# Two runs of matmuls joined, and a later start of the exponentials, ahead of a gated cross-attention pipeline

## The chip, the cores and the metric

The kernel runs on one core of a Trainium2 chip. The metric is the device time of one execution in microseconds (us). A core has five engines that run side by side and meet at semaphores: TensorE (PE in the profile; its weight loads are listed apart as PEld), VectorE (DVE), ScalarE (ACT), GpSimd (POOL) and SyncE (SP), which here only issues DMA transfers. Each engine works through its own list of instructions.

## The reference, cut to what matters

All data are float32. `x` has 4 sequences of 2048 tokens with 512 features, and `ctx_768` has 4 contexts of 77 tokens with 384 features.

```python
q = split_heads(layernorm(x) @ Wq)          # 16 heads of 64
k = split_heads(context @ Wk); v = split_heads(context @ Wv)
attn = softmax(einsum('bhid,bhjd->bhij', q, k) * SCALE)
out = einsum('bhij,bhjd->bhid', attn, v)     # heads joined again
x = x + tanh(g_xattn[0]) * (out @ Wo + bo)
x = x + tanh(g_ffn[0]) * (layernorm(x) @ W[idx] + b[idx])   # idx = argmax of logits + gumbel noise
```

The kernel uses that the context is short. For every batch it forms M = Wq·Kᵀ and VO = V·Wo once, so that scores are x·M and the attention output is p·VO.

## The kernel before, in words

**Tiling.** The 8192 tokens are cut into 16 groups of 512, four groups to a sequence. For each group the kernel computes the scores, the softmax, the attention output with its residual and the feed-forward layer. The groups are pipelined: while one group's scores run on TensorE, the softmax of that group or the one before runs on ScalarE, VectorE and GpSimd.

**Seven products.** Every large matmul is done by the class `Seven` (line 452): a 2x2 block product with seven block products in place of eight. `product(s)` issues the matmuls of step s (line 482), and `post(s)` takes the result out of PSUM. There are two ways to do that: a `keep` step is a copy on ScalarE (line 488, with a bias line 492), and an added step is an addition on VectorE (line 506). Steps with the same result slot r write to the same PSUM bank one after the other, so the later one needs the copy of the earlier one first. In the usual order, steps 0 and 2 share slot 0: step 2 accumulates onto what step 0 left, after ScalarE has copied it. Each float32 product of 128x256 shows as two MATMUL instructions.

**Scores.** The scores of a group are made by three such objects: `s0` for the first two pairs of key chunks (8 MATMUL instructions in a step), `s1` for the next two (8) and `s2` for the last one (4). For group 1, six steps of `s0` come first, in an order of their own (`SHORT`, line 460). Then a loop of seven turns issues one step of `s1` and one of `s2` in each turn; behind its first turn it issues the seventh step of `s0`. In `SHORT`, steps 0, 2, 3 and 5 are copied by ScalarE, and steps 1, 4 and 6 are added by VectorE.

**VO.** `build_vo(p, engines)` (line 334) makes VO of two heads, 2p and 2p+1. It has six results (three chunks of rows by two heads), each with one 64-row matmul of 512 columns, which shows as two MATMUL instructions, twelve for a pair (line 343). Each result is scaled on its way from PSUM into a staging slot, by VectorE (line 346) or ScalarE (line 348); the letters of `engines`, taken in turn, say which: "DDA" gives the third and the sixth result to ScalarE, "D" none. Four DMA transfers, issued by SyncE, then take the pair to DRAM (lines 352 and 353). Heads from 2 on rotate through five staging slots, so head 13 takes the slot of head 8. `load_vo(0)` (line 359) reads batch 0's part of VO back, once all are stored.

**Softmax.** For group 0, `head_max(0, h)` on VectorE (lines 544 and 546) makes the negated maxima of a set of four heads. `exps(0, n0, n1)` on ScalarE (line 552) makes 64 exponentials, 16 for each set; those of set h need `head_max(0, h)`. `head_sum` (VectorE, line 559) and `head_scale` (GpSimd, line 563) follow, and then `p_columns` (VectorE, line 572).

**PSUM and order.** Seven PSUM banks are handed out in rotation (`bank`, line 88). While `s0` keeps its first bank, six rotate. The kernel is written under a manual schedule: the order of the calls is the order on each engine. The stage around the change is written by hand on lines 764 to 791: VO of pairs 3 to 7 stands between the steps of group 1's scores, while the exponentials of group 0 fill ScalarE. The list `e` says how many exponentials come by the end of each turn of the loop. The last of the 64 stand ahead of `s1.post(0)` on ScalarE (lines 791 to 797).

Of the kernel before, what the change touches and what calls it, by code (L numbers as in the profile page):

```python
# [19 lines left out]
def flamingo_block_kernel(  # L20
# [34 lines left out]
    NT, D = x.shape  # L55
# [32 lines left out]
    def bank(name):  # L88
        return pm.tile([P, 512], F32, tag="mm", name=name)
# [29 lines left out]
    def weight_sum(w, n, engine=None):  # L119

        to, a, b_, op = ((5, 0, 3, ALU.subtract), (3, 3, 2, ALU.add), (4, 3, 0, ALU.subtract),
                         (6, 1, 4, ALU.subtract))[n]
        (engine or nc.gpsimd).tensor_tensor(flat(w[:, to]), flat(w[:, a]), flat(w[:, b_]), op)
# [65 lines left out]
    def by_chunk(t):  # L189

        return t.rearrange("p (a q e) -> p q a e", a=NA, e=32)

    def chunked(t):
        return t.rearrange("p (q a e) -> p q a e", a=NA, e=32)
# [61 lines left out]
    def v_cols(p, at, n):  # L256
        return vT_f[:, ds(p * BP + at, n)] if p < 7 else wf_f[:, ds(6 * D + at, n)]
# [72 lines left out]
    def stage_of(h):  # L330

        return vo_st[h if h < 2 else 2 + (h - 2) % (len(vo_st) - 2)]

    def build_vo(p, engines):
        n = 0
        for c in range(3):
            r = min(P, BP - c * P)
            for hh in range(2):
                stg = stage_of(2 * p + hh)
                hr = ts(hh, DH)  # L340
                ps = bank("ps_vo")

                nc.tensor.matmul(ps, v_cols(p, c * P, P)[hr], wo[hr, p, :], start=True, stop=True)  # L343
                src, dst = by_chunk(ps[:r, :]), chunked(stg[:r, c, :])
                if engines[n % len(engines)] == "D":
                    nc.vector.tensor_scalar(dst, src, tgx[:r], None, ALU.mult)
                else:
                    nc.scalar.activation(dst, src, AF.Copy, scale=tgx[:r])
                n += 1
        for hh in range(2):  # L350
            d, stg = vo_d[2 * p + hh], stage_of(2 * p + hh)
            nc.sync.dma_start(out=d[0 : 2 * P].rearrange("(c r) e -> r c e", r=P), in_=stg[:, 0:2])
            nc.sync.dma_start(out=d[2 * P :], in_=stg[: BP - 2 * P, 2])
# [5 lines left out]
    def load_vo(bi):  # L359
        src = vo_d.rearrange("h (r b k) e -> (h r) b k e", b=B, k=NK)[:, bi]  # L360
        for o, c in ((0, 0), (1, 0), (1, 1), (0, 1)):
            nc.sync.dma_start(out=vo[:, BLK[o, c]], in_=src[:, ts(c, KH), ts(o, D // 2)])
# [174 lines left out]
    def head(i, h):  # L537
        return sc[i][:, h, :, :J]
# [3 lines left out]
    def head_max(i, h):  # L542
        mx = stat[:, ds((16 + h) * NG, NG)]
        nc.vector.tensor_reduce(mx, head(i, h), AX.X, ALU.max)  # L544
        nmx[h] = small.tile([P, NG], F32, tag=f"nmx{h}", name="nmx")
        nc.vector.tensor_tensor(nmx[h], mx, norms[i].down, ALU.mult)  # L546

    def exps(i, n0, n1):

        for n in range(n0, n1):  # L550
            h, g = n // NG, n % NG
            nc.scalar.activation(head(i, h)[:, g, :], head(i, h)[:, g, :], AF.Exp,  # L552
                                 scale=norms[i].up[:, g : g + 1], bias=nmx[h][:, g : g + 1])
# [3 lines left out]
    def head_sum(i, h):  # L557
        sums[h] = sm = small.tile([P, NG], F32, tag=f"sm{h}", name="sm")
        nc.vector.tensor_reduce(sm, head(i, h), AX.X, ALU.add)  # L559
        nc.vector.reciprocal(sm, sm)  # L560

    def head_scale(i, h):
        nc.gpsimd.tensor_tensor(head(i, h), head(i, h), sums[h].unsqueeze(2).to_broadcast([P, NG, J]),  # L563
                                ALU.mult)
# [115 lines left out]
    def centre_wf(wfr, c):  # L680
        nc.gpsimd.tensor_tensor(wfr[:, c, :], wfr[:, c, :], wf_mean, ALU.subtract)
        for o in range(2):
            nc.gpsimd.tensor_scalar(chunked(wf[:, BLK[o, c // 2], c % 2, :]), by_chunk(wfr[:, c, :])[:, ts(o, 2)],
                                    tgf, None, ALU.mult)
# [79 lines left out]
    head_max(0, 0)  # L764
    build_vo(3, "AAD")
    head_max(0, 1)
    exps(0, 0, 8)
    e = (8, 16, 24, 32, 41, 50, 57)
    for s in range(6):
        s0.product(s)  # L770
        s0.post(s)
        if s < 2:
            centre_wf(wfr, 2 * s)
            centre_wf(wfr, 2 * s + 1)
        if s == 2:
            weight_sum(wf, 0)
            weight_sum(wf, 1)
        if s == 3:
            weight_sum(wf, 2)
        if s < 4:  # L780
            build_vo(4 + s, "DDA" if s < 2 else "D")
        if s < 2:
            head_max(0, 2 + s)
        exps(0, e[s], e[s + 1])
        if s == 3:
            weight_sum(wf, 3)
            load_vo(0)
        if 3 <= s:
            head_sum(0, s - 3)
            head_scale(0, s - 3)  # L790
    exps(0, 57, 64)
    for s in range(7):
        s1.product(s)
        s2.product(s)
# [32 lines left out]
    for i in range(1, NGRP):  # L827
# [69 lines left out]
        for s in range(7):  # L897
# [12 lines left out]
            if 1 <= s:  # L910
                e = (0, 10, 20, 32, 44, 56, 64)
# [225 lines left out]
```

## Time and profile before

| what | value |
|---|---|
| median of three runs | 1242.3 us (1242.0 to 1243.12) |
| the profiled execution, whole time | 1242.8 us |
| its span, first to last instruction | 1241.0 us, so 1.8 us lie around it |
| TensorE busy | 1231.3 us (99% of the span) |
| VectorE, GpSimd, ScalarE busy | 904.9, 894.0, 684.9 us |
| mean granted TensorE clock | 0.998 |

The table is read as follows. A busy share is an average over all stages. The engine with the highest share need not set the end in each of them, and busy TensorE is not TensorE at its peak, because the ends of matmuls are modelled. So the chain of work that ended last is read next, and then the instructions of the one stage that the change touches, from about 87 to 133 us.

### The profile page before, as it was taken

The page shows a single profiled execution, that of the slowest core. Times are in us where ns is not written, and L with a number is a line of the kernel's source. Part 1 is how long each engine was busy: PE and PEld are TensorE (multiplying, and loading weights), DVE is VectorE, ACT ScalarE, POOL GpSimd, SP SyncE. Part 2 cuts the span into 40 slices and gives each one's busy share as a digit, 9 for nine tenths or more (in the row PEclk, how much of TensorE's full clock was granted, in tenths as well). Part 3 has the DMA queues.
Part 4 walks back from the last instruction along what each step waited for, and adds up shares of the span by engine and source line. Part 5 has one row for each costly group of instructions (what it writes and reads, how often), then busy time and mean ns, then how long its engine had stood idle before and what let it go on. Part 6 is the DMA issues. An engine that isn't in the chain of part 4 may idle for free.

```text
span 1241.0 us, 17016 instructions
## 1 busy us (share of the span) xinstructions
PE 1231.3 (99%) x5704; PEld 1063.2 (86%) x5704; DVE 904.9 (73%) x1843; ACT 684.9 (55%) x1970; POOL 894.0 (72%) x493
## 2 busy tenths in 40 slices
PE   9999999999999999999999999999999999999997
PEld 6676888888888888888888888888888888888886
DVE  6788977666877766677776767776776877666576
ACT  4648545548273564827356482745638274563824
POOL 5559885758957775785968778575977877585666
PEclk9999999999999999999999999999999999999999
DMA  9868200314023030304006030202304121010102
GB/s 269 324 194 286 32 1 1 68 47 107 1 62 92 1 69 1 69 22 125 8 1 153 1 69 1 56 14 85 68 1 111 43 52 17 1 35 1 35 1 68
DMA packets 94486, 80.28 MB, mean 65 GB/s; under 512 B 3888, under 2 KB 81584, under 8 KB 94400
## 3 DMA queue, kind: packets, MB, share of 16 engines
q1 hardware_dynamic: 92128, 76.61, 24.2%
q10 hardware_dynamic: 1664, 1.47, 0.4%
q0 software_dynamic: 608, 1.13, 0.2%
q8 instruction: 45, 0.74, 0.2%
q14 instruction: 41, 0.34, 0.1%
HBM read 44.07 MB, written 35.13 MB: 64 GB/s over the span
## 4 chain that ended last, share of the span: by engine, by line
PE 96%; DVE 2%; ACT 0%; DMA 0%; POOL 0%; issue 0%; DVEq 0%
PE ps_s L482 39%; PE ps_a L482 37%; PE ps_f L482 15%; PE ps_kv L269 2%; PE ps_vo L343 2%; PE ps_m L307 1%; DVE s L377 1%; ACT t L606 0%; DMA m<-in_Wk_dram 0%; POOL r L405 0%; DVE t L424 0%; DVE r L400 0%; DVE y L424 0%; DVE snap L506 0%; DVE y L602 0%
## 5 line engine op out<-in xcount | busy, mean ns | idle before, releaser
L482 PE MATMUL ps_a<-pT,vo 128*128 128x256 f32 x2240 | 486.2, 379 | 0.0
L482 PEld LDWEIGHTS ps_a<-pT,vo 128*128 128x128 f32 x2240 | 425.6, 190 | 57.9
L552 ACT ACTIVATE s<-s,nmx,up 128x77 f32<-128x77 f32 x1024 | 355.8, 445 | 1.6 <-DVE nmx L546 1.6
L444 POOL TENSOR_TENSOR pT<-pT 128x1280 f32<-128x1280 f32 x64 | 185.8, 2904 | 171.1 <-PE ps_a L482 164.4
L482 PE MATMUL ps_s<-tq,m 128*128 128x256 f32 x1280 | 290.6, 380 | 0.0
L482 PEld LDWEIGHTS ps_s<-tq,m 128*128 128x128 f32 x1280 | 242.6, 190 | 36.0 <-issue 1.5
L488 ACT COPY snap<-ps_s 128x512 f32<-128x512 f32 (+1 forms) x188 | 93.6, 514 | 291.1 <-DVE t L424 131.1
L482 PE MATMUL ps_s<-xc,m 128*128 128x256 f32 x960 | 221.1, 379 | 0.0
L482 PEld LDWEIGHTS ps_s<-xc,m 128*128 128x128 f32 x960 | 182.2, 190 | 27.4 <-issue 1.2
L563 POOL TENSOR_TENSOR s<-s,sm 128x1232 f32<-128x1232 f32 x64 | 145.2, 2269 | 47.4 <-DVE sm L560 47.3
L506 DVE TENSOR_TENSOR snap<-snap,ps_s 128x512 f32<-128x512 f32 (+1 forms) x141 | 83.7, 594 | 126.6 <-PE ps_s L482 121.6
L482 PE MATMUL ps_f<-tq,wf 128*128 128x256 f32 x512 | 118.3, 379 | 0.0
L572 DVE STREAM_TRANSPOSE pT<-s 128x512 f32<-128x512 f32 x160 | 101.1, 678 | 15.8 <-POOL s L563 15.8
L444 POOL TENSOR_TENSOR tq<-xc,tq 128x512 f32<-128x512 f32 x64 | 85.2, 1332 | 34.9 <-PE ps_f L482 32.4
L405 POOL TENSOR_TENSOR r<-r,neghalf 32x16 f32<-32x16 f32 (+1 forms) x33 | 93.1, 2831 | 21.9 <-DVE r L400 21.3
L482 PEld LDWEIGHTS ps_f<-tq,wf 128*128 128x128 f32 x512 | 97.3, 190 | 13.2
L559 DVE TENSOR_REDUCE sm<-s 128x16 f32<-128x1232 f32 x64 | 91.5, 1429 | 21.9 <-ACT s L552 21.9
L535 DVE STREAM_TRANSPOSE s<-snap 128x512 f32<-128x512 f32 x156 | 99.9, 685 | 6.1 <-ACT snap L488 3.8
L544 DVE TENSOR_REDUCE ps_st<-s 128x16 f32<-128x1232 f32 x64 | 92.4, 1444 | 2.1
L482 PE MATMUL ps_f<-xc,wf 128*128 128x256 f32 x384 | 90.7, 379 | 0.0
L444 POOL TENSOR_TENSOR tq<-xc 128x512 f32<-128x512 f32 x64 | 81.4, 1272 | 7.2 <-DVE xc L419 5.8
L488 ACT COPY snap<-ps_f 128x512 f32<-128x512 f32 x63 | 36.9, 585 | 86.8 <-PE ps_f L482 86.8
(142 smaller groups left out, 1183.5 us busy)
## 6 DMA issues: line engine op xcount, KB each, us to landing
xg<-in_x_dram SPq DMA_DIRECT2D x64, 256.0 KB, 5.9
out_dram<-y SPq DMA_DIRECT2D x60, 256.0 KB, 4.8
vo<-vo_d SPq DMA_DIRECT2D x16, 640.0 KB, 5.6
m<-m_d SPq DMA_DIRECT2D x12, 640.0 KB, 4.2
vo_d<-vo SPq DMA_DIRECT2D x14, 512.0 KB, 4.2
m_d<-vo SPq DMA_DIRECT2D x4, 960.0 KB, 6.4
wq<-in_WqT_dram SPq DMA_DIRECT2D x8, 256.0 KB, 4.9
wq<-in_Wo_dram SPq DMA_DIRECT2D x1, 2048.0 KB, 13.7
```

The costliest lines, as they stand in the source:

```text
L269: nc.tensor.matmul(ps[:, :BJ], w[:, c, ts(p, P)], cR[:, c].rearrange("p b j -> p (b j)"), start=(c == 0), stop=(c == NCC - 1))
L405: nc.gpsimd.tensor_tensor(r, r, neghalf[:32, : r.shape[1]], ALU.pow)
L444: (engine or nc.gpsimd).tensor_tensor(self.at[name], self.at[a], self.at[b_], op)
L482: nc.tensor.matmul(self.ps[r][:, n, :], self.w(blk, c, pair), self.cols(cname, c), start=(first and n == 0 and c == 0), stop=(c == h - 1), ...
L488: nc.scalar.copy(dst, self.ps[r])
L506: nc.vector.tensor_tensor(c, c, self.ps[r], ALU.add)
L535: nc.vector.transpose(key_chunk(sc[i], k), cols.rearrange("p (g h r) -> p g h r", h=HA, r=R))
L544: nc.vector.tensor_reduce(mx, head(i, h), AX.X, ALU.max)
L552: nc.scalar.activation(head(i, h)[:, g, :], head(i, h)[:, g, :], AF.Exp, scale=norms[i].up[:, g : g + 1], bias=nmx[h][:, g : g + 1])
L559: nc.vector.tensor_reduce(sm, head(i, h), AX.X, ALU.add)
L563: nc.gpsimd.tensor_tensor(head(i, h), head(i, h), sums[h].unsqueeze(2).to_broadcast([P, NG, J]), ALU.mult)
L572: nc.vector.transpose(pT[i].all[:, k, :].rearrange("p (g h r) -> p g h r", h=HA, r=R), key_chunk(sc[i], k))
```

## The change

Only the stage on lines 764 to 791 is changed.

- Behind step 0 of group 1's scores, VO of pair 4 is no longer made. Steps 0 and 1 of `s0` follow each other on TensorE.
- Behind step 1, VO of pair 4 and then of pair 5 are made, both with the pattern "DDA". Two exponentials stand ahead of pair 4 on ScalarE, six between the pairs and two behind them. `head_max(0, 2)` stands behind both pairs.
- Behind step 2, two exponentials come first. Then comes VO of pair 6, now with the pattern "DDA" instead of "D", so that two of its six results go to ScalarE. Then come `head_max(0, 3)` and eight exponentials.
- Pair 7 stays behind step 3 with the pattern "D".
- The exponentials are spread in another way: 4 stand ahead of the loop (8 before), 18 are issued by the end of the turn of step 1, 28 by that of step 2, 38, 48 and 56 by those of steps 3, 4 and 5 (before: 16, 24, 32, 41, 50 and 57 by the ends of the six turns). The rest, now 8 and before 7, follows the loop as before.

The number of instructions of each kind is the same, but for two scalings that move from VectorE to ScalarE.

```diff
-    exps(0, 0, 8)
-    e = (8, 16, 24, 32, 41, 50, 57)
+    exps(0, 0, 4)
+    e = (4, 8, 18, 28, 38, 48, 56)
     for s in range(6):
         s0.product(s)
         s0.post(s)
...
-        if s < 4:
-            build_vo(4 + s, "DDA" if s < 2 else "D")
-        if s < 2:
-            head_max(0, 2 + s)
-        exps(0, e[s], e[s + 1])
+        if s == 1:
+            exps(0, 8, 10)
+            build_vo(4, "DDA")
+            exps(0, 10, 16)
+            build_vo(5, "DDA")
+            head_max(0, 2)
+            exps(0, 16, e[2])
+        else:
+            e0 = e[s]
+            if s == 2:
+                exps(0, e0, e0 + 2)
+                e0 += 2
+            if s in (2, 3):
+                build_vo(4 + s, "DDA" if s == 2 else "D")
+            if s == 2:
+                head_max(0, 3)
+            exps(0, e0, e[s + 1])
...
-    exps(0, 57, 64)
+    exps(0, 56, 64)
     for s in range(7):
         s1.product(s)
         s2.product(s)
```

## The prediction

> **What bounds the kernel now.** I read the page's busy shares first, then the chain that ended last in order of time, then the timeline of ScalarE in the changed stage. The chain is TensorE nearly throughout, so only what TensorE waits for, or spends itself, counts. Its pieces (start, us, what) in the stage:
>
> ```profile
> 48.20 7.72 PE ps_vo L343 x36
> 87.33 2.77 PE ps_vo L343 x12
> 90.10 1.93 PE ps_s L482 x8
> 92.03 2.77 PE ps_vo L343 x12
> ...
> 108.90 23.51 PE ps_s L482 x108
> 132.41 30.22 PE ps_a L482 x140
> 162.63 10.36 PE ps_f L482 x48
> ```
>
> The reader is to see that short runs are dear: a matmul costs 7.72 / 36 = 0.214 us in a long VO run and 10.36 / 48 = 0.216 in a long run of products, but twelve in a run of their own take 2.77 (not 2.57) and eight take 1.93 (not 1.73). Each start of a run costs 0.20 us.
>
> The timeline of ScalarE has start, duration, line, tiles, count, and in brackets idle time with who ended it:
>
> ```profile
> 93.97 0.69 ACT L348 ACTIVATE vo<-ps_vo,tg 128x512 f32<-128x512 f32 x1
> 94.88 0.68 ACT L348 ACTIVATE vo<-ps_vo,tg 64x512 f32<-64x512 f32 x1 [0.21 <-PE ps_vo L343]
> 98.67 0.69 ACT L348 ACTIVATE vo<-ps_vo,tg 128x512 f32<-128x512 f32 x1 [0.38 <-PE ps_vo L343]
> 99.62 0.68 ACT L348 ACTIVATE vo<-ps_vo,tg 64x512 f32<-64x512 f32 x1 [0.26 <-PE ps_vo L343]
> 106.16 0.59 ACT L488 COPY snap<-ps_s 128x512 f32<-128x512 f32 x1
> 106.64 5.59 ACT L552 ACTIVATE s<-s,nmx,up 128x77 f32<-128x77 f32 x16
> 118.09 0.57 ACT L488 COPY sn<-ps_s 128x512 f32<-128x512 f32 x1
> 121.22 0.58 ACT L488 COPY sn<-ps_s 128x512 f32<-128x512 f32 x1 [1.35 <-PE ps_s L482]
> ```
>
> ScalarE idles 0.85 us between 88.42 and 118.09. The copy at 118.09 is `s1.post(0)`, ending at 118.66. TensorE's timeline says when it is needed:
>
> ```profile
> 112.39 4.48 PE L482 MATMUL ps_s<-xc,m 128*128 128x256 f32 x20
> 116.71 5.34 PE L482 MATMUL ps_s<-tq,m 128*128 128x256 f32 x24
> ```
>
> The 24 are steps 1 and 2 of `s1` and `s2`. Step 2 of `s1` starts behind twelve of them, at 116.71 + 12 x 0.216 = 119.30, and needs that copy. So the cover is only 0.64 us. This is the narrow place.
>
> **The change part by part.** *Two starts of runs go.* Between VO of pair 3 and the long run there are nine starts now and seven afterwards: -2 x 0.20 = -0.40 us, all on the path. New starts by the same rows: steps 0 and 1 at 90.03, pairs 4 and 5 at 90.03 + 1.93 + 1.73 = 93.69, step 2 at 93.69 + 2.77 + 2.57 = 99.03, pair 6 at 100.96, step 3 at 103.73, pair 7 at 105.66, the long run at 108.43 (108.83 now).
>
> *VectorE.* A scaling takes 4.03 / 6 = 0.67 us. In a VO run the two heads come together: the first two results are there 1.16 us after the start (102.52 against 101.36 in pair 6 now), the next two at 2.01, the last two at 2.9. VectorE, done with `s0.post(1)` at 94.5 (step 1 ends at 93.7, 0.2 later its addition starts, 0.63), has pair 4's four scalings done at 97.5 and pair 5's at 100.2, `head_max(0, 2)` (1.43 + 0.17) at 101.8. It waits for pair 6 until 102.12 and so keeps up. With six banks in rotation, pair 5's first two matmuls want, at 96.46, the banks that pair 4's first scalings leave at 95.5 and 96.2. That fits by 0.2; if the weight load waits, it costs at most the 0.20 of a start. Bounds 0 and 0.2; I take 0.1, the margin being as large as the cost. Pair 6's two scalings off VectorE buy nothing, as it waits for pair 7's first result (105.66 + 1.16 = 106.82) anyway.
>
> *Queues.* Pair 4's and 5's stores are issued one to three us later. Head 13 in pair 6 wants the slot of head 8, whose last store is issued at about 97.6. Stores of this size landed after 2.3 to 3.8 us in the stage, so at 101.4 at the latest, before the 102.8 of the first scaling. Pair 7's last store comes 0.4 earlier, and with it `load_vo(0)`: no gain, since the loaded part is first read on TensorE at 132. GpSimd gets no new step before the last `head_scale`.
>
> *ScalarE, the step that decides.* An exponential costs 0.343 us in sequence ((5.59 - 0.445) / 15, with 0.445 the mean of one), a scaling 0.575 (four from 88.42 to 90.72), a copy 0.48 (106.16 to 106.64). Behind pair 6's run start (100.96), the last result comes at 103.86. Walking the queue up to there: four exponentials end at 92.1, copy, four and two more by 94.7; the third result of pair 4 comes only at 95.7 (idle 1.0), the sixth at 96.6 (idle 0.3); six exponentials, two scalings, two exponentials to 101.1, a copy, two exponentials to 102.3; pair 6's third result at 102.97 (idle 0.7), its sixth at 103.86 (idle 0.3). Idle time is 2.4 us, not 0.85, and there are two scalings more. From 103.86: scaling 0.575, 44 exponentials 15.1, the copies of steps 3 and 5 0.96, so `s1.post(0)` starts at 120.5 (118.09 now) and ends at 121.07. Behind `s1.post(0)` ScalarE has slack again (1.35 us of idle before 121.22 now).
>
> TensorE wants that copy at 119.30 - 0.40 = 118.90. It gets going after 121.07, plus 0.05 for the semaphore (the chain's issue pieces are 0.02 to 0.07) and up to 0.20 for the weight load, which can't be hidden after a wait. I take 0.25 in all, the row of a run's start being the nearest; with both at nothing the wait is 2.17. So a wait of 2.4 us appears where there was none: +2.4.
>
> *What the later end of the exponentials does next.* The last `head_sum`, `head_scale`, `p_columns` move by 2.4, and TensorE behind them by 2.0, so relative to it they lose 0.4. The nearest need is step 6 of `s1` at 129.66 now, on a bank that VectorE leaves at 127.5: cover 2.1, so nothing.
>
> *Sum*: -0.40 + 2.42 + 0.1 = +2.1 us. Against the profiled execution that is 1242.8 + 2.1 = 1244.9; that execution lies 0.5 above the median, so the forecast is 1242.3 + 2.1 = 1244.4. No change from which a measurement of this kernel could tell it is about 0.2%, or 2.5 us (1244.8): the forecast lies just inside.
>
> **The clock.** TensorE never stands still for microseconds in the stages before the end, so the one row is the end. The stretches, with granted clock in the third column from the right:
>
> ```profile
> 1232.00:1233.00 1.00, 0.63 (x3) 0.20 (x2) 0.96 (x4) 0.92 (x5) 1.00 (x2) 1.00 0.00 0
> 1234.00:1235.00 1.00, 0.00 (x0) 0.00 (x0) 0.90 (x2) 0.00 (x0) 0.92 (x2) 1.00 0.46 104
> 1235.00:1236.00 1.00, 0.00 (x0) 0.00 (x0) 0.87 (x2) 0.00 (x0) 0.90 (x1) 0.52 0.85 170
> ```
>
> The last matmul ends at 1232.63 and the clock is halved from about 1235.04, 2.4 us later: just the length of the wait above. The price of a fall is bounded by the start of the kernel: the first 48 projections take 13.66 us against 12.64 for the next 48, 1.02 lost, and the six warm-up matmuls take 2.93 against 1.29 at full rate, 1.64 lost. Bounds 1.0 and 2.7; I take 1.7, in the middle.
>
> The Trainium skill, "TensorE: Matmul & The Clock Gate", section "HAM oscillation — how this bites in real kernels", asks for no TensorE gap beyond some 3.4 us, and counts the half clock in windows of that length. By it this gap costs nothing and the sum stays at 1244.4; an estimate from its figure for one window at half clock is 1.7 lost. The row, with a fall after 2.4 us, differs and speaks against the change.
>
> **Rivals.** *The clock falls in the new wait.* For it: the 2.4 us above. Against it: the moment of counting may lie unfavourably, and a fall needs nearly the whole gap. It decides once the gap passes about 2.4 us in one count. 1244.4 + 1.7 = 1246.1, slower.
>
> *The cover holds.* If step 2 of `s1` didn't wait for that copy, or ScalarE made up its idle time, the two starts are all: 1242.3 - 0.4 = 1241.9. For it: no TensorE wait on ScalarE is seen now. Against: 118.66 lies ahead of 119.30 now, so none could be seen.
>
> *A staging store is late.* Pair 6's sixth result on ScalarE belongs to head 13. If head 8's store lands after 103.86, every later exponential slips by the excess; from 0.4 us on the whole is slower than 0.2%, and with 1 us it is 1245.4. Against: that needs 6.3 us to land, and 3.8 is the longest in the stage.
>
> **How the numbers follow.** Wait without a fall of the clock 0.47, own range 1243.7 to 1245.2, of which 0.36 lies inside 0.2% and 0.11 above it, where ScalarE is later by another 0.4; clock falls 0.36; cover holds 0.10; late store 0.05; a gain beyond 2.5 us, for which no row speaks, 0.02. Faster 0.02, same 0.36 + 0.10 = 0.46, slower 0.11 + 0.36 + 0.05 = 0.52. The range leaves out the held cover below and about 0.08 above: 1242.9 to 1246.8 (the top is 1244.4 with a fall at 2.4, between the 1.7 taken and its bound of 2.7).
>
> **What would show it.** Right: vo runs of 24 in the chain; ScalarE's copy of `s1.post(0)` near 120.5; a TensorE gap of about 2.4 us ahead of step 2 of `s1`, released by ACT; everything later shifted by the same 2.1. Wrong: no such gap, a granted clock under 1.00 near 122, or ScalarE idle behind pair 6.

## The result and the profile after

The changed kernel takes 1245.71 us (median of 13 executions, 1244.4 to 1247.48), the one before 1243.12 us (13 executions, 1242.0 to 1243.73). The ratio is 1.0025, with a 95% interval of 1.0018 to 1.0033. So the change costs some 3 us (2.6 by the medians, 3.1 by the ratio). The profiled execution after has a span of 1243.9 us, 2.9 us more than that of before.

Single executions of one kernel differ by a microsecond or more at their start, far ahead of the change: the first 48 projections took 13.66 us in the profile of before, 12.83 in that of after and up to 14.89 in the profiles further down. So the profiles are compared over one stretch, called the stage here. It runs from the first matmul of pair 3's VO to the first matmul of step 1 of group 0's feed-forward layer. Both points are read from TensorE's timeline. (In the chain, a piece that nothing released begins at the modelled end of the piece before it: for the kernel before 0.07 and 0.17 us later than the matmuls at these two points.)

The chain of the profile after in order of time (start, us, what):

```profile
86.57 2.78 PE ps_vo L343 x12
89.35 3.65 PE ps_s L482 x16
93.00 5.39 PE ps_vo L343 x24
98.39 1.93 PE ps_s L482 x8
100.32 2.82 PE ps_vo L343 x12
...
119.87 0.47 ACT sn L488
120.35 0.04 issue
120.39 14.90 PE ps_s L482 x60
135.30 30.22 PE ps_a L482 x140
165.51 10.36 PE ps_f L482 x48
```

The two joined runs are there, and they cost what long runs cost. But the chain now goes through ScalarE, which releases TensorE at 120.39. The ends of the stage in TensorE's timeline of before:

```profile
87.26 2.85 PE L343 MATMUL ps_vo<-wq 64*128 64x512 f32 x12
164.19 2.11 PE L482 MATMUL ps_f<-tq,wf 128*128 128x256 f32 x9
```

And of after:

```profile
86.50 2.85 PE L343 MATMUL ps_vo<-wq 64*128 64x512 f32 x12
167.08 3.62 PE L482 MATMUL ps_f<-tq,wf 128*128 128x256 f32 x16
```

The stage lasts 76.93 us before and, from unrounded starts, 80.57 us after, 3.64 us more. The accounts close: the execution after came to pair 3 by 0.75 us sooner, lost 3.64 us in the stage, and from there to the end both take the same (1076.8 us).

TensorE's timeline of after inside the stage (start, duration, line, tiles, count, and in brackets the idle time ahead, counted from the modelled end of the matmul before, with who ended it):

```profile
115.60 2.75 PE L482 MATMUL ps_s<-tq,m 128*128 128x256 f32 x12
120.39 4.54 PE L482 MATMUL ps_s<-tq,m 128*128 128x256 f32 x12 [2.04 <-ACT sn L488]
124.77 2.75 PE L482 MATMUL ps_s<-xc,m 128*128 128x256 f32 x12
```

The 24 matmuls of steps 1 and 2, one run before, are cut in two by a wait for ScalarE's copy. And the second twelve take 4.54 us where the first take 2.75. The stretches of the same profile (length, then busy time and count of PE, PEld, DVE, ACT, POOL, then granted clock, DMA share, GB/s) say why:

```profile
118.00:119.00 1.00, 0.35 (x2) 0.00 (x0) 0.00 (x0) 1.00 (x4) 0.62 (x1) 1.00 1.08 336
119.00:120.00 1.00, 0.00 (x0) 0.00 (x0) 0.10 (x1) 1.00 (x4) 0.00 (x0) 1.00 1.05 353
120.00:121.00 1.00, 0.61 (x2) 0.58 (x3) 1.00 (x1) 1.00 (x4) 0.00 (x0) 0.85 1.04 362
121.00:122.00 1.00, 1.00 (x4) 0.73 (x4) 0.59 (x2) 0.35 (x2) 0.23 (x1) 0.50 1.07 359
122.00:123.00 1.00, 1.00 (x4) 0.82 (x3) 0.00 (x0) 0.00 (x0) 1.00 (x1) 0.50 1.15 322
123.00:124.00 1.00, 1.00 (x4) 0.82 (x3) 0.00 (x0) 0.06 (x1) 1.00 (x2) 0.50 1.23 185
124.00:125.00 1.00, 1.00 (x6) 0.81 (x6) 0.93 (x2) 0.56 (x2) 1.00 (x2) 0.94 1.24 177
```

From about 120.7 to 124.1 the granted clock is 0.50: a row then counts four matmuls, with those that its edges cut, and six at full clock.

ScalarE's own timeline of after shows where it lost its time:

```profile
94.95 0.69 ACT L348 ACTIVATE vo<-ps_vo,tg 128x512 f32<-128x512 f32 x1 [0.98 <-PE ps_vo L343]
95.85 0.68 ACT L348 ACTIVATE vo<-ps_vo,tg 64x512 f32<-64x512 f32 x1 [0.21 <-PE ps_vo L343]
102.27 0.69 ACT L348 ACTIVATE vo<-ps_vo,tg 128x512 f32<-128x512 f32 x1 [0.64 <-PE ps_vo L343]
103.17 0.68 ACT L348 ACTIVATE vo<-ps_vo,tg 64x512 f32<-64x512 f32 x1 [0.21 <-PE ps_vo L343]
119.77 0.57 ACT L488 COPY sn<-ps_s 128x512 f32<-128x512 f32 x1
```

It idles 0.98 us ahead of pair 4's third result, and 0.64 ahead of pair 6's third, which it didn't scale before; with the two gaps of 0.21 that is 2.04 us, against 0.85 before. The copy of step 0 of `s1` starts 33.27 us behind pair 3's VO in the timelines (119.77 - 86.50); before it was 30.83 (118.09 - 87.26).

### The profile page after: what moved, and what is told of

It is laid out like the page before. It is cut to its first block, busy times and chain, and to the rows that moved or that the text cites. A ratio compares the mean times of both kernels' runs of the same rounds, so it can differ in the third digit from the quotient of the medians.

```text
span 1243.9 us, 17018 instructions
## 1 busy us (share of the span) xinstructions
PE 1232.0 (99%) x5704; PEld 1066.2 (86%) x5704; DVE 904.0 (73%) x1841; ACT 686.0 (55%) x1972; POOL 894.0 (72%) x493
## 4 chain that ended last, share of the span: by engine, by line
PE 95%; DVE 2%; ACT 2%; DMA 0%; POOL 0%; issue 0%; DVEq 0%
PE ps_s L482 38%; PE ps_a L482 37%; PE ps_f L482 15%; PE ps_kv L269 2%; PE ps_vo L343 2%; PE ps_m L307 1%; ACT s L552 1%; DVE s L377 1%; ACT t L606 0%; DMA m<-in_Wk_dram 0%; POOL r L405 0%; DVE t L424 0%; DVE r L400 0%; DVE y L424 0%; DVE snap L506 0%
```

## The experiments

The theory to test first was that the copy of step 0 of `s1` comes too late and nothing else, and that the clock falls because of the wait. The table gives all runs. All times are counted from the first matmul of pair 3's VO, and all but those of before are differences to before, in us. "Last sum" is the start of the last `head_sum` of group 0, which follows the last exponential. "Attention" is the first matmul of group 0's attention output; the expectations below end their stage there (45.08 us before, by the chain). "Stage" is the stretch defined above, and "lateness" is how much later TensorE is 16 matmuls further on, and stays to its last matmul.

| kernel | last sum | attention | stage | lateness | clock at half in the stage | ratio to before, 95% interval |
|---|---|---|---|---|---|---|
| before | 30.97 | 44.99 | 76.93 | | no | |
| after | +2.43 | +3.64 | +3.64 | +3.64 | yes | 1.0025 (1.0018 to 1.0033) |
| after_again | +2.44 | +3.64 | +3.64 | +3.64 | yes | 1.0027 (1.0018 to 1.0036) |
| e1_copy_first | +3.18 | +1.26 | +2.95 | +3.06 | no | 1.0024 (1.0014 to 1.0034) |
| e2_pair6_vector | +1.01 | +0.53 | +0.79 | +0.89 | no | 1.0008 (0.9999 to 1.0017) |
| e3_pair6_alone | +1.42 | +0.94 | +1.20 | +1.30 | no | 1.0011 (1.0002 to 1.0020) |
| e4_filled_gap | +2.43 | +1.95 | +2.21 | +2.31 | no | 1.0017 (1.0007 to 1.0026) |
| e5_half_wait | +3.18 | +1.26 | +2.95 | +3.06 | no | 1.0024 (1.0014 to 1.0033) |
| e7_exps_behind_copy | +0.74 | 0.00 | +0.52 | +0.62 | no | 1.0004 (0.9995 to 1.0013) |
| e8_joined_refilled | -0.70 | -0.31 | -0.31 | -0.31 | no | 0.9996 (0.9987 to 1.0005) |

The six kernels that wait for the second chain described below lose another 0.10 us between the last two points: sixteen matmuls behind a wait take 3.72 us and not 3.62, twelve 2.86 and not 2.75.

**The copy ahead of the last exponentials.** The change, with this edit:

```diff
-    exps(0, 56, 64)
...
             s1.post(0)
             s2.post(0)
+            exps(0, 56, 64)
```

> Edit: the change, with the last eight exponentials of group 0 put behind the first copies of s1 and s2 on ScalarE. The stage from the start of VO of pair 3 to the start of the attention took 45.08 us before and 48.73 after the change. Theory (ScalarE reaches the copy of step 0 of s1 too late): the copy starts 8 x 0.343 = 2.7 us earlier, no TensorE wait is left at step 2 of s1, the clock stays at 1.00, and only the two saved starts of runs are left: stage 45.08 - 0.40 = 44.7 us, time 0.4 us under before. Rival (the joined runs wait by themselves, on banks or on VectorE): a wait of some 2 us stays and the stage is 47 us or more.

The wait at step 2 did go: steps 1 and 2 are one run again. But the time didn't come back. TensorE's timeline of this kernel:

```profile
116.24 5.34 PE L482 MATMUL ps_s<-tq,m 128*128 128x256 f32 x24
130.69 2.86 PE L482 MATMUL ps_s<-tq,m 128*128 128x256 f32 x12 [1.34 <-DVE sn L506]
167.03 3.72 PE L482 MATMUL ps_f<-tq,wf 128*128 128x256 f32 x16 [1.33 <-POOL tq L444]
```

Two waits stand further down, 1.34 us for VectorE and 1.33 us for GpSimd, and the clock stays at 1.00 behind both. So the first half of the theory, that only the copy counts, fell. The chain of this kernel says what the waits come from:

```profile
118.51 2.76 ACT s L552 x8
121.29 1.45 DVE sm L559
...
123.17 2.27 POOL s L563
125.46 0.50 DVE pT L572
...
142.25 3.54 ACT s L552 x10
...
165.70 1.28 POOL tq L444
166.98 0.04 issue
167.03 8.90 PE ps_f L482 x40
```

It starts at group 0's last exponential and runs on through its sum, its scaling and its transposes, then through group 1's maxima and exponentials, to the column sums of the feed-forward layer on GpSimd. It never touches TensorE for 46 us. The moved exponentials end 0.75 us later than after the change (3.18 against 2.43), because the two copies (0.47 and 0.27) now stand ahead of them. So the edit cured one chain and fed another, which starts on the same engine.

**Half of it.** The change, with only four exponentials moved:

```diff
-    exps(0, 56, 64)
+    exps(0, 56, 60)
...
             s2.post(0)
+            exps(0, 60, 64)
```

> Edit: the change, with only the last four exponentials put behind the first copies of s1 and s2. Theory: the copy comes 1.37 us earlier, TensorE waits 2.2 - 1.37 = 0.8 us, and a wait so short does not halve the clock; stage 45.08 - 0.40 + 0.85 = 45.5 us, time 0.4 us over before. If the clock falls for waits of this length too, the stage is 47.2 us. If the copy is not what is waited for, the stage stays at 48.7 us.

The wait at step 2 was 0.67 us where 0.8 was foreseen, and the clock stayed. But the stage is the same as in the run before to the hundredth, 2.95 us over before. The last exponential ends at the same place in both, and that sets the stage. How TensorE's waits on the way are divided (0.67, 0.41 and 1.32 us here, 1.34 and 1.33 there) doesn't matter.

**Pair 6 by VectorE alone.** The change, with this edit:

```diff
-                build_vo(4 + s, "DDA" if s == 2 else "D")
+                build_vo(4 + s, "D")
```

> Edit: the change, but pair 6 scaled by VectorE alone, as before. Theory: ScalarE saves the two scalings and the waits for them, but then waits for step 3 (there 0.1 us after its run ends), so the copy of step 0 of s1 starts 1.4 us earlier than after the change; TensorE wants it 0.4 us earlier than before and waits 0.8 us; clock 1.00 throughout; stage 45.08 - 0.40 + 0.85 = 45.5 us, time 0.4 us over before. Rival (the joined runs alone make the wait): the wait stays at 2.0 and the stage at 47 to 48.7 us.

The wait at step 2 is 0.62 us, and the attention starts 0.53 us later than before. The theory had 0.45, the rival about 2 us or more. So the joined runs do not make the long wait by themselves, but they are not free: with the exponentials spread as in the change, ScalarE idles 1.87 us and not 0.85 (0.98 and 0.21 at pair 4's results, 0.68 ahead of the copy of step 3), and the last sum comes 1.01 us later. How much of that is due to the joined runs and how much to the spread, this run does not separate.

**Pair 6's scalings alone.** The kernel before, with this edit:

```diff
-            build_vo(4 + s, "DDA" if s < 2 else "D")
+            build_vo(4 + s, "DDA" if s < 3 else "D")
```

> Edit: the kernel before, with the one part that pair 6 is scaled by both engines (DDA). Theory (two chains that begin on ScalarE): the last exponential ends 1.15 + 0.3 = 1.45 us later than before. The copy of step 0 of s1 then ends at about 120.1 where step 2 wants it at 119.30, so TensorE waits 0.8 to 0.9 us; and the chain that goes on from the last exponential (sum, scaling, transposes, group 1's maxima and exponentials, the sums of the feed-forward layer's columns) had only 0.23 us to spare, so by the feed-forward layer's step 1 TensorE is 1.2 us late in all. Clock 1.00 in the stage. Time 1.2 us over before. Rival (only the copy counts): 0.9 us over before, and no wait at the feed-forward layer. Rival (joining the runs is the cause): no change from before.

Here the last sum is 1.42 us later and step 1 of the feed-forward layer 1.20 us, both as expected, with no run joined. The rival in which only the copy counts had 0.9 us and no wait further on: the attention is 0.94 us late, but the delay grows to 1.30 behind step 1, for which TensorE waits on GpSimd. This part (1.42) and that of the rest of the change (1.01) add up to the 2.43 of the whole.

**The second chain alone.** The kernel before, with its last exponentials moved behind the copies:

```diff
-    exps(0, 57, 64)
...
             s1.post(0)
             s2.post(0)
+            exps(0, 57, 64)
```

> Edit: the kernel before, with its last seven exponentials of group 0 put behind the first copies of s1 and s2 on ScalarE; nothing else. Theory (second chain): the copy comes 2.4 us earlier, so it can't be waited for, but the last exponential ends 0.75 us later (two copies stand ahead of it), which exceeds the 0.23 us that the second chain had to spare, so TensorE waits 0.5 us ahead of step 1 of group 0's feed-forward layer, for GpSimd; time 0.5 us over before. Rival (the copy is the only place where ScalarE matters): no wait anywhere, time as before.

The copy comes early here, no run is joined, and every scaling stays where it was. Still TensorE waits, in one place:

```profile
162.75 1.89 PE L482 MATMUL ps_f<-xc,wf 128*128 128x256 f32 x8
165.00 3.72 PE L482 MATMUL ps_f<-tq,wf 128*128 128x256 f32 x16 [0.35 <-POOL tq L444]
```

The last sum is 0.74 us later, and step 1 starts 0.52 us later, as the theory had it. (The 0.35 us in the row count from the modelled end of the matmul before.) So the second chain had 0.22 to 0.23 us to spare in the kernel before. All six experiments that slip and keep the clock agree on it: the stage grows by the slip of the last sum less that much (3.18 to 2.95 twice, 1.01 to 0.79, 1.42 to 1.20, 2.43 to 2.21, 0.74 to 0.52). The time of this kernel by itself (1.0004, with 1 inside the interval) couldn't have told it.

**The wait filled with work.** The change, with unused matmuls in TensorE's wait; nothing is left out, and they add 1.73 us of work:

```diff
     for s in range(7):
+        if s == 2:
+            fill = bank("ps_w")
+            for _ in range(4):
+                nc.tensor.matmul(fill[:, :T2], xc[1]("B11", 0)[:, :P], xc[1]("B11", 0), start=True, stop=True)
         s1.product(s)
```

> Edit: the change, with four unused matmuls of 256 columns (eight MATMUL instructions, 1.73 us) put into TensorE's wait ahead of step 2 of s1; it adds work and leaves the order of all else. Theory (the clock is halved because TensorE stands still for about 2 us): the clock stays at 1.00, step 2 of s1 starts as late as after the change (33.8 us behind the start of pair 3's VO), and the stage takes 48.73 - 1.7 = 47.0 us; the time falls by 1.7 us against the change, to 1.5 us over before. Rival (the slow matmuls behind the wait come from something else, such as the transfers or the weights): stage 48.7 us and time as after the change or more.

TensorE's timeline, with the added matmuls on line 808:

```profile
118.06 2.75 PE L482 MATMUL ps_s<-tq,m 128*128 128x256 f32 x12
120.65 1.89 PE L808 MATMUL ps_w<-xc 128*128 128x256 f32 x8
122.86 2.86 PE L482 MATMUL ps_s<-tq,m 128*128 128x256 f32 x12 [0.31 <-ACT sn L488]
```

Its stretches:

```profile
122.00:123.00 1.00, 0.69 (x4) 0.29 (x3) 0.63 (x1) 1.00 (x4) 0.00 (x0) 1.00 1.09 351
123.00:124.00 1.00, 1.00 (x5) 0.90 (x6) 0.96 (x2) 0.81 (x3) 0.00 (x0) 1.00 1.11 353
124.00:125.00 1.00, 1.00 (x6) 0.87 (x6) 0.09 (x1) 0.11 (x1) 0.77 (x1) 1.00 1.09 351
```

Step 2 starts as late as after the change, 33.89 us behind pair 3's VO in both. But the clock stays at 1.00 and its twelve matmuls take 2.86 us, not 4.54, although the transfers run at 351 to 353 GB/s, within the 185 to 362 of the slow stretches there. So the slow matmuls come from the idle TensorE and not from its neighbours. The attention starts 1.69 us sooner than after the change, where 1.7 was expected. Of that, 1.33 us remain in the end, because the second chain now sets it (2.31 us over before, not 1.95). The times of all executions agree: this kernel's median is 2.28 us over before, that of the changed kernel below 3.67.

**The changed kernel again.** No edit.

> The changed kernel as it is, once more, for the clock. Theory (the clock is judged in stretches of 3.4 us whose start is unrelated to the kernel, and falls when most of one is idle): the same wait of 2.0 to 2.2 us ahead of step 2 of s1, and either again 3.4 us at half clock behind it and a stage of 48.7 us, or none and a stage of 47.0 us; in the second case TensorE waits another 0.3 us at the feed-forward layer's step 1. The times of single runs then lie in two bands some 1.4 us apart, blurred by about 1 us from the kernel's start. Rival (the clock falls in every run): always 48.7 us.

The wait was 2.04 us once more and the clock fell once more, as two of the stretches show:

```profile
121.00:122.00 1.00, 0.50 (x2) 0.48 (x3) 0.99 (x1) 1.00 (x3) 0.00 (x0) 1.00 1.09 353
123.00:124.00 1.00, 1.00 (x4) 0.81 (x3) 0.00 (x0) 0.00 (x0) 1.00 (x1) 0.50 1.11 341
```

It fell 1.4 us behind the end of the wait here and 0.3 us behind it in the first profile, so the moment is not tied to the wait. Yet the stage is 80.57 us in both. It can hardly fall in every execution: both profiles show it, but two of the 24 times of the changed kernel (1244.16 and 1244.4; the others are 1245.48 and more) lie less than 2.5 us above the fastest of before (1242.0), and with a fall 3.64 are lost. In how many it falls stays open; two clear bands were not seen.

**A kernel that keeps the joined runs.** The change, with the stage's lists written anew:

```diff
-    build_vo(3, "AAD")
+    build_vo(3, "AADADD")
...
-    exps(0, 0, 4)
-    e = (4, 8, 18, 28, 38, 48, 56)
+    exps(0, 0, 5)
+    e = (5, 14, 21, 33, 43, 52, 60)
...
         if s == 1:
-            exps(0, 8, 10)
             build_vo(4, "DDA")
-            exps(0, 10, 16)
+            exps(0, 14, 17)
             build_vo(5, "DDA")
             head_max(0, 2)
-            exps(0, 16, e[2])
+            head_max(0, 3)
+            exps(0, 17, 21)
         else:
-            e0 = e[s]
-            if s == 2:
-                exps(0, e0, e0 + 2)
-                e0 += 2
             if s in (2, 3):
-                build_vo(4 + s, "DDA" if s == 2 else "D")
-            if s == 2:
-                head_max(0, 3)
-            exps(0, e0, e[s + 1])
+                build_vo(4 + s, "D")
+            exps(0, e[s], e[s + 1])
...
-    exps(0, 56, 64)
+    exps(0, 60, 64)
```

> Edit: the change's two joined runs, but with pair 6 scaled by VectorE alone, one scaling of pair 3 moved from ScalarE to VectorE (AADADD), the maxima of the sets 2 and 3 both behind pair 5, and the exponentials put where ScalarE idled (5 ahead of the loop, 14, 21, 33, 43, 52 and 60 by the ends of the turns). Theory (both chains begin on ScalarE, and the runs' starts are TensorE's own cost): the last exponential ends 0.8 us earlier than before against the start of pair 3's VO, neither chain is waited for, the clock stays at 1.00, and the stage from pair 3's VO to the attention takes 45.08 - 0.40 = 44.7 us; time 0.4 us under before. Rival (a joined run makes TensorE wait for banks): a wait on VectorE inside the VO of pairs 4, 5 or 7, stage 45.1 us or more.

The chain is TensorE alone again:

```profile
86.52 2.77 PE ps_vo L343 x12
89.29 3.65 PE ps_s L482 x16
92.94 5.39 PE ps_vo L343 x24
...
107.78 23.51 PE ps_s L482 x108
131.29 30.22 PE ps_a L482 x140
```

From pair 3's VO to the attention it is 131.29 - 86.52 = 44.77 us, against 45.08 before: 0.31 of the 0.40 us. The joined VO run takes 5.39 and not 5.34, and pair 7's run 2.82 and not 2.78, some 0.05 us each. The last sum is 0.70 us earlier than before, where 0.8 was expected of the last exponential, and TensorE waits for neither chain. Several things were moved at once here, so this profile shows that the joined runs can be kept without either chain being late, and not which of the moves does it. The median is 1242.31 us against 1242.62 in the same session. That is the expected direction, but the ratio 0.9996 (0.9987 to 1.0005) can't be told from no change. It is plainly faster than the changed kernel (1246.29 there).

## Why the prediction came out as it did

**The time** says less than it seems. 1245.71 us lies inside the stated range, nearer to the rival with a fall of the clock (1246.1) than to the forecast (1244.4). But before itself was measured 0.8 us higher here than in the three runs on which the forecast stands, and the rise of 2.6 to 3.1 us lies between the forecast's 2.1 and the rival's 3.8. What happened is told by the profiles.

**The starts of runs** were right: 3.65 and 5.39 us for the joined runs, 3.66 and 5.34 foreseen. Up to `s1` they save 0.35 us, not 0.40. **ScalarE's queue**, the step that was said to decide, was right to a few hundredths: the copy was put 33.24 us behind pair 3's VO (120.5 - 87.26) and came at 33.27. The four idle times were foreseen as 1.0, 0.3, 0.7 and 0.3 us (2.3 in all, and not the 2.4 of the text, which nothing else uses) and measured as 0.98, 0.21, 0.64 and 0.21. **The wait** was foreseen as 2.42 us and measured as 2.20: step 2 starts 1.85 us later than before, and would have started 0.35 sooner. (The 2.04 in the row count from a modelled end.) The missing 0.22 is the restart: 0.04 us of issue lies between the copy's end and the matmul, not the 0.25 taken. The matmuls behind the wait cost another 0.10, so that the wait by itself makes TensorE -0.35 + 2.20 + 0.10 = 1.95 us late, as the kernel with the filled wait shows at the attention.

**The clock** is where the likeliest case failed. The prediction took the wait without a fall as likeliest (0.47) and the fall as its nearest rival (0.36). The rival is what both profiles of the changed kernel show, and "a granted clock under 1.00 near 122" was among the prediction's own signs of being wrong. The fall cost 3.64 - 1.95 = 1.69 us, as half of the 3.41 us at half clock would (1.71). The 1.7 foreseen hit that, but as the middle of bounds from 1.0 to 2.7, and so with some luck. The step that failed is "a fall needs nearly the whole gap", with 2.4 us as the point of decision: 2.04 us of idle time was enough twice, and 1.34, 0.67 and 0.62 were not. The 2.4 us came from one row at the end of the kernel, and such a row is one draw. In the ten profiles the clock fell between 2.04 us (the second chain alone) and 5.31 us (the kernel that keeps the joined runs) behind the last matmul. The Trainium skill, "TensorE: Matmul & The Clock Gate", section "HAM oscillation — how this bites in real kernels", asks for no gap beyond some 3.4 us; here a shorter one tripped the gate, and the measurement decides. What the page says of the length of a window (3413 ns, in its section "What's actually happening") agrees: the half clock lasted 3.41 us in both profiles.

**What the later end of the exponentials does next** was wrong, though it didn't show. That step named step 6 of `s1` as the nearest need, with a cover of 2.1 us, and costed the slip at nothing. That cover was read rightly: in the run with the copy first, step 6 started 1.15 us later than before, so that the slip of 3.18 had used up some 2.03 first. But there is a nearer need some 35 us further on, the feed-forward layer's step 1, with only 0.23 us of cover. It hides behind the clock's fall in the changed kernel. Without a fall it makes TensorE 2.31 us late (the filled wait), close to the forecast of 2.1 by coincidence: the forecast reached it by the copy's wait, which gives 1.95.

**Stores, banks and VectorE** held as foreseen. No wait on a staging store or on `load_vo` was seen, and a joined VO run lost 0.05 us, not the 0.1 taken.

## What to carry to other kernels

When one engine is busy throughout, its timeline shows no waits, and so it also shows no slack: for each thing that will come later, follow its consumers until one reaches the bounding engine, and subtract the two times there, not only at the first consumer. Here two chains left the same engine with 0.64 and 0.23 us to spare, and mending the one through the copy alone made the other later. The wait of TensorE of 2.20 us here cost another 1.69 us through the clock, and unused matmuls in it cost less than standing still (2.31 us over before, not 3.64); but it was cheaper to fill the other engine's idle time so that the wait didn't arise (0.31 under before).

## What was not expected of the hardware

A gap of 2.04 us in TensorE's work halved its clock for 3.41 us in both profiles of the changed kernel, 1.69 us of lost time. The moment at which the clock falls isn't tied to the gap (0.3 and 1.4 us behind its end in two executions) but to a grid that the traces' records of the clock show: in both profiles it fell 116.05 us, or 34 x 3.413, behind its first rise, and the falls at the ends of the ten kernels lie 360 to 362 such steps behind it. Where 2.04 us of the step before such a point were idle, it fell (the second chain alone, at its end); where 1.91 us were, it didn't (the kernel that keeps the joined runs, one step ahead of its fall at the end). Both are counted from modelled ends of matmuls, in one profile each.

The kernel's first 48 projections took 12.83 to 14.89 us in ten profiles whose work there is the same, and this blurs the times of single executions by as much as most of the differences looked for here. The same records say what goes with it: the clock's first rise comes 4.61 to 9.20 us into the kernel, and in every profile the projections take 12.64 us, the time of the next 48, and half of the time from their start to that rise, to 0.05 us. So they go at half rate until then, although the rows show a clock of 1.00 there: the record begins with that rise.
